# A four-layer graph network: row products summed by VectorE out of PSUM, early blocks' turned sums kept, weighted products in one run

## The chip, the cores and the metric

The kernel runs on one core of a Trainium2 chip. A core has TensorE (PE in the profile, its weight loads PEld), VectorE (DVE), ScalarE (ACT), GpSimd (POOL) and SyncE (SP), whose queue issues most of the transfers. The metric is the device time of one execution in microseconds; lower is better.

## What is computed

The input is x, 3327 nodes of 64 features, and adj, a 3327 x 3327 matrix of weights with many zeros. Four layers follow each other, each of the form x = layernorm(x + f(x)). Layer 1 is a hyperbolic graph layer; for it the part that matters here reads

```python
x_tan = logmap0(x)
adj_att = sigmoid(left + right.T) * adj
x_local = logmap(x[:, None, :], x[None, :, :])
support = einsum('ij,ijd->id', adj_att, x_local)
out = proj(expmap(support, x))            # needs, for each node i, dots such as
x = layernorm(x + out)                    # sum_d x[i,d]*m[i,d] and sum_d m[i,d]**2
```

Here m is a weighted sum over the neighbours. Layer 2 is `x = tanh(concat([adj @ x, x]) @ W)`, twice; layer 3 counts the neighbours of each node and weights the last hundred of them.

## The kernel before

The nodes are padded to 3328 = 26 blocks of 128. Two blocks, one of each half of the nodes, lie side by side as 128 columns, so there are 13 pairs ("slots" 2g and 2g+1 for pair g). `adjT` is streamed from HBM in row blocks of 128 x 3328, 1664 KB each; seven of them stay in SBUF (`kept`).

**near_sphere** is layer 1's main loop: 104 tiles, each with a product on TensorE (L1387), Arctan on ScalarE (L1396), products with the attention on VectorE (L1407 to L1411) and a sum on TensorE (L1431). Its sums go by ScalarE (L1437) into `mT`, node along the free axis. In its last tiles POOL multiplies a half of mT with riT (the rows of x turned, L1614) into xm, and makes small statistics of [128, 26]; TensorE turns blocks 0 to 5 of mT back to node-major, centred, in the PSUM tile pq_early (L1627), whose squares (sq_e) and last columns (t_e) ScalarE takes (L1632, L1636). VectorE makes the other half of xm (L1643) and the row sums of sq_e (L1644).

**near_end** ends layer 1. TensorE turns blocks 6 to 12 (m_and_t, L1702), then sums xm by node with 26 matmuls against but_last, two columns wide, into the PSUM tile pe (p_of, L1722). ScalarE squares the turned blocks (L1716) and copies them into x2 (m_out, L1712). VectorE takes pe (L1768) and runs a long chain of operations on [128, 26], through one Tanh (L1806) and two roots (L1839) on ScalarE, to the factors alpha, beta and beta_c (L1870, L1871, L1880). Meanwhile TensorE turns blocks 0 to 5 once more, and makes x times layer 2's weight (x_w, from w_x) and m times the weight (m_w, from w_m), both by `times` (L1742). `x_out` (L1748) copies x_w into lj by ScalarE. VectorE at last makes lj = alpha * m_w + beta * x_w by groups of blocks (L1877 to L1879: pair 0; pairs 1 to 3; 12; 4 to 7; 8 to 11), then x2 (L1884 to L1886).

**layers** begins with layer 2's first product: for each row block, eight matmuls (16 records) into four PSUM accumulators cnt, taken by turns, two matmuls each (L517, in the order third, first, fourth, second bank of the four). It needs lj of that block and the block's adjT. Four blocks (at_l) are loaded ahead; after them SP's queue has bt_l (one buffer, in the pool `more`), then at_l again. A tile of masks, `carry`, `tm` and `more` lie in SBUF where near_end's tiles lay.

What sets the order: between `tc.manual_schedule` marks each named engine runs its instructions in the order of the program's text; SP's queue runs in its own. Each engine is in order, so an instruction that waits holds everything behind it on that engine. A pool opened with `reuse_waits="tile"` waits tile by tile for what lay in its place. Two engines reading one PSUM tile take turns in the order of the text (L1732's reads follow L1716's squares). PSUM has eight banks: before, four belong to the pool l1w (x_w, m_w and the like), one to l1t (pe), three to l1m (pm); layer 2's accumulators take the upper four.

Of the kernel before, what the change touches and what calls it, by code (L numbers as in the profile page):

```python
# [19 lines left out]
P = 128  # L20
# [62 lines left out]
def kernel(  # L83
# [1093 lines left out]
    with tc.tile_pool(name="l1", bufs=1) as l1:  # L1177

        def l1_stat(name):
            return l1.tile([P, NB], F32, name=name)  # L1180

        aa, g1, ga, xn, rxn, gs, gs2, gk, lpn, aav, gsp = (
            l1_stat(name)
            for name in ("aa", "g1", "ga", "xn", "rxn", "gs", "gs2", "gk", "lpn", "aav", "gsp")
# [104 lines left out]
        def near_sphere(mT, ljT_0, xm, sq_e, t_e):  # L1289
# [3 lines left out]
            with tc.tile_pool(name="n1", bufs=1, reuse_waits="tile") as n1, tc.tile_pool(  # L1293
# [235 lines left out]
                with tc.manual_schedule(  # L1529
# [69 lines left out]
                    for t in range(len(tiles)):  # L1599
# [12 lines left out]
                        if t == len(tiles) - 4:  # L1612
                            of = slice(0, 2 * CW)
                            nc.gpsimd.tensor_tensor(xm[:, of], mT[:, of], riT[:, of], ALU.mult)  # L1614
                            gp = nc.gpsimd

                            gp.tensor_scalar(gs, g1, MIN_NORM, ANGLE_LEAD, ALU.max, ALU.mult)
                            gp.tensor_tensor(gk, gs, ga, ALU.mult)
                            gp.tensor_scalar(gsp, g1, -0.5, None, ALU.mult)
                            gp.tensor_tensor(gsp, gsp, gs, ALU.mult)  # L1620
                            gp.tensor_tensor(gs2, gs, gs, ALU.mult)
                            gp.tensor_scalar(aav, aa, 1.0 / D, LN_EPS, ALU.mult, ALU.add)
# [8 lines left out]
                        if t == len(tiles) - 2:  # L1631
                            nc.scalar.activation(  # L1632
                                sq_e.rearrange("p (a k h) d -> p a k (h d)", a=2, k=3),
                                pm[..., :P], AF.Square,
                            )
                            nc.scalar.copy(  # L1636
                                t_e.rearrange("p (a k h) -> p a k h", a=2, k=3), pm[..., P:]
                            )
                    stt(inv_s, vq[:, 1], -0.5 / 0.9, r2[:, 1], op0=ALU.mult, op1=ALU.mult)
                    stt(rxn, r2[:, 0], -0.5, inv_s, op0=ALU.mult, op1=ALU.mult)  # L1640
                    vec(xn, aa, rxn, ALU.mult)
                    for of in (slice(c * CW, (c + 1) * CW) for c in (2, 3)):
                        vec(xm[:, of], mT[:, of], riT[:, of], ALU.mult)  # L1643
                    nc.vector.tensor_reduce(lpn[:, :12], sq_e, axis=AX.X, op=ALU.add)  # L1644

        def near_end(mT, ljT, xm, t_e, x2):
# [4 lines left out]
            with tc.tile_pool(name="l1e", bufs=1) as l1e, tc.tile_pool(  # L1651
                name="l1w", bufs=4, space=PSUM
            ) as l1w, tc.tile_pool(name="l1t", bufs=1, space=PSUM) as l1t, tc.tile_pool(
# [57 lines left out]
                def m_out(g, n):  # L1711
                    nc.scalar.copy(halves_of(x2[:, slots(g, n)]), m_of(g))  # L1712
# [5 lines left out]
                pe = l1t.tile([P, NBH, 2], F32, name="pe")  # L1718

                def p_of(first, last):  # L1720
                    for k in range(first, last):
                        nc.tensor.matmul(  # L1722
                            pe[:, k], xm[:, k * P : (k + 1) * P], but_last,
                            start=True, stop=True,
                        )
# [27 lines left out]
                p_of(0, NBH)  # L1753
                squares(6, 3)
                squares(9, 3)
                squares(12, 1)
# [10 lines left out]
                p = pe.rearrange("p n h -> p (n h)")  # L1767
                vec(k, p, gs, mul)  # L1768
                vec(gp, p, gsp, mul)
# [7 lines left out]
                m_and_t(0, 3)  # L1777
# [11 lines left out]
                m_and_t(3, 3)  # L1789
                last_x = in_bank("x_w_12")  # L1790
                times(last_x, ljT, w_x, *fours[3])
                ka = of(mul, k, aa, "ka")
# [14 lines left out]
                nc.scalar.copy(w_m, second[:, :P])  # L1807
                warm_e = st("warm")
                nc.scalar.activation(warm_e[:, :1], ones, AF.Sqrt)
                m_out(0, 3)  # L1810
# [33 lines left out]
                x_out(xs[0], *fours[0])  # L1844
                x_out(xs[1], *fours[1])
# [10 lines left out]
                m_out(3, 3)  # L1856
                nc.scalar.copy(w3_dg, second[:, P : 2 * P])
                x_out(last_x, *fours[3])
                rest_x = in_bank("x_w_8")
                mw = {b: in_bank(f"m_w_{b}") for b in (0, 3, 1, 2)}  # L1860
                times(mw[0], mT, w_m, *fours[0])
                times(rest_x, ljT, w_x, *fours[2])
                x_out(rest_x, *fours[2])
                for b in (3, 1, 2):
                    times(mw[b], mT, w_m, *fours[b])
# [232 lines left out]
        with tc.If(n_below == 0) as norms:  # L2098
            with ExitStack() as arm:
                with tc.tile_pool(name="n1m", bufs=1) as n1m:  # L2100
                    mT = n1m.tile([P, HALF], F32, name="mT")
                    ljT_0 = n1m.tile([P, HALF], F32, name="ljT_0")
                    sq_e = n1m.tile([P, 12, D], F32, name="sq_e")
                    t_e = n1m.tile([P, 12], F32, name="t_e")

                    xm = x2.rearrange("p n d -> p (n d)")
                    near_sphere(mT, ljT_0, xm, sq_e, t_e)
                    blocks = blocks_ahead(arm)
                    near_end(mT, ljT_0, xm, t_e, x2)
                layers(x2, xc, True, *blocks)  # L2110
# [43 lines left out]
```

## Time and profile before

| what | us |
|---|---|
| median of three runs (498.72 to 500.65) | 500.58 |
| profiled execution, its own time | 499.99 |
| its span, first to last instruction | 498.2 |
| TensorE busy in the span | 480.3 (96%) |
| VectorE busy | 349.5 (70%) |
| ScalarE busy | 266.1 (53%) |
| POOL busy | 192.1 (39%) |
| near_sphere's last product on VectorE ends (L1409) | 189.4 |
| near_end's chain begins (L1768) | 195.47 |
| layer 2's first matmul (L517) | 205.14 |
| layer 2's first pass ends | 288 |

A line of a timeline gives start, duration, engine, line of the kernel, operation, tiles written and read, shapes, number of instructions merged, and in brackets the idle time before it with what ended it. A line of waits gives who waited for whom, the total, the number of times and the longest. A line of the table by stretch gives, after each engine's busy time, the granted TensorE clock (1.00 is full), the transfers' share of the DMA engines, and GB/s.

### The profile page before, as it was taken

The numbers are of one execution on the slowest core, as the hardware profiler recorded it, in microseconds if no ns is written. First come the engines' busy times: TensorE is split into PE (matmuls) and PEld (weight loads), VectorE is DVE, ScalarE is ACT, GpSimd is POOL, SyncE is SP. The second block draws the span as 40 slices with busy tenths as digits, with TensorE's granted clock in tenths as the row PEclk, the third lists the DMA queues.
The fourth block names the chain that finished last, engine by engine and source line by source line (L and its number), as shares of the span: only waits on it lengthen the run. The fifth ranks groups of instructions, "written<-read, shape, count | busy, mean of one in ns | idle before, by whom it ended". The sixth has DMA issues, their size and how long they took to land. (4 is left out here: it accounts for less than half of the span.)

```text
span 498.2 us, 7727 instructions
## 1 busy us (share of the span) xinstructions
PE 480.3 (96%) x2865; PEld 220.4 (44%) x2865; DVE 349.5 (70%) x602; ACT 266.1 (53%) x377; POOL 192.1 (39%) x171
## 2 busy tenths in 40 slices
PE   7999999999999999999999999999999999999992
PEld 4733333333333338643333353333345554455551
DVE  6788888878888887995363322656239998788744
ACT  4799999999999985300000000000016885657541
POOL 4299999989999991000000000000242154000000
PEclk9799999999999998999999999999999999999996
DMA  9888988887888278899999019998987699949001
GB/s 278 340 284 285 328 265 274 273 272 259 283 274 277 72 285 312 365 402 428 424 425 379 0 22 393 430 362 325 414 337 236 224 331 364 392 162 357 3 1 43
DMA packets 34202, 139.20 MB, mean 279 GB/s; under 512 B 11263, under 2 KB 13041, under 8 KB 29035
## 3 DMA queue, kind: packets, MB, share of 16 engines
q1 hardware_dynamic: 30603, 137.41, 73.8%
q0 software_dynamic: 1216, 0.63, 0.6%
q10 hardware_dynamic: 2336, 0.58, 0.6%
q8 instruction: 24, 0.39, 0.3%
q14 instruction: 23, 0.19, 0.1%
HBM read 136.93 MB, written 1.04 MB: 277 GB/s over the span
## 5 line engine op out<-in xcount | busy, mean ns | idle before, releaser
L1365 POOL TENSOR_TENSOR sg<-sg,at 128x832 f32<-128x832 f32 x88 | 131.4, 1517 | 7.7 <-ACT sg L1360 3.7
L517 PE MATMUL cnt<-at_l,lj 128*64 128x416 f32 x496 | 90.8, 515 | 0.8 <-DMA at_l<-in_adjT 0.8
L1360 ACT ACTIVATE sg<-lb,rb 128x1664 f32<-128x1664 f32 (+1 forms) x53 | 88.1, 1664 | 0.0
L1387 PE MATMUL pq<-riT,ljT 64*128 64x416 f32 x416 | 87.4, 536 | 0.2
L1431 PE MATMUL acc<-v,lj 128*64 128x416 f32 x416 | 85.2, 525 | 0.0
L1396 ACT ACTIVATE pq<-pq 128x832 f32<-128x832 f32 x104 | 83.8, 851 | 1.8 <-issue 1.6
L630 ACT ACTIVATE x<-cnt 128x416 f32<-128x416 f32 x8 | 4.1, 517 | 144.7 <-PE cnt L517 144.7
L669 ACT ACTIVATE w<-cnt 128x416 int16<-128x416 f32 x136 | 63.9, 522 | 25.3 <-PE cnt L651 23.8
L1411 DVE SCALAR_TENSOR_TENSOR v<-pq,sg 128x832 f32<-128x832 f32 x52 | 53.3, 1025 | 19.0 <-ACT pq L1396 18.6
L464 POOL DMA_DIRECT2D t_rows<-tb x4 | 2.7, 720 | 151.0 <-DVE tb L462 151.0
L1387 PEld LDWEIGHTS pq<-riT,ljT 64*128 64x128 f32 x416 | 35.5, 186 | 49.8 <-ACT pq L1396 30.6
L517 PEld LDWEIGHTS cnt<-at_l,lj 128*64 128x64 f32 x496 | 34.3, 137 | 51.0 <-issue 48.4
L882 PE MATMUL acc<-w,s 128*128 128x416 bf16 x208 | 53.1, 339 | 0.0
L1431 PEld LDWEIGHTS acc<-v,lj 128*64 128x64 f32 x416 | 26.1, 136 | 52.3 <-issue 48.2
L667 DVE TENSOR_SCALAR w<-cnt 128x416 int16<-128x416 f32 x72 | 41.6, 587 | 10.0 <-PE cnt L651 7.8
L517 PE MATMUL cnt<-kept,lj 128*64 128x416 f32 x224 | 41.6, 514 | 0.0
L651 PE MATMUL cnt<-mask,tri 128*128 128x416 bf16 x136 | 35.5, 339 | 1.8 <-ACT w L669 0.9
L368 DVE TENSOR_SCALAR mask<-ah 128x1664 bf16<-128x1664 f32 x34 | 35.5, 1060 | 2.3 <-DMA ah<-in_adjT 2.3
L1408 DVE SCALAR_TENSOR_TENSOR pq<-pq,sg 128x416 f32<-128x416 f32 x52 | 31.2, 600 | 1.8
L445 DVE TENSOR_SCALAR tm<-at_l 128x1664 bf16<-128x1664 f32 x16 | 15.7, 1023 | 22.9 <-PE t L452 20.9
L1407 DVE SCALAR_TENSOR_TENSOR v<-pq,sg 128x416 f32<-128x416 f32 x52 | 30.2, 581 | 0.0
L1035 POOL DMA_DIRECT2D out<-hid x1 | 0.5, 502 | 74.5 <-DVE hid L1040 74.5
(320 smaller groups left out, 523.5 us busy)
## 6 DMA issues: line engine op xcount, KB each, us to landing
at_l<-in_adjT SPq DMA_DIRECT2D x27, 1664.0 KB
at<-in_adjT SPq DMA_DIRECT2D x44, 832.0 KB
ah<-in_adjT SPq DMA_DIRECT2D x34, 832.0 KB
kept<-in_adjT SPq DMA_DIRECT2D x7, 1664.0 KB
bt_l<-in_adjT SPq DMA_DIRECT2D x6, 1664.0 KB
lb<-lf_rows SPq DMA_DIRECT2D x2, 384.0 KB
mask<-t_rows SPq DMA_DIRECT2D x34, 3.2 KB
ljT<-ljT SPq DMA_DIRECT2D x4, 128.0 KB
```

Source lines behind the costliest of these rows:

```text
L368: nc.vector.tensor_scalar(mask[q], ahead.pop(q), 0.0, None, ALU.not_equal)
L517: nc.tensor.matmul(acc[c][h * D : (h + 1) * D, :], hw[:, slot(jb), :], blocks[jb][:, o : o + CW], start=c not in begun, stop=last, skip_gr ...
L651: nc.tensor.matmul(cnt[c][e], tri, mask[q][:, of], start=True, stop=True, skip_group_check=True,)
L667: nc.vector.tensor_scalar(to, of, 0.0, None, ALU.max)
L669: nc.scalar.activation(to, of, AF.Relu)
L882: nc.tensor.matmul(acc[h, c][:, e, :], s12[:, slot(jb)].rearrange("p t d -> p (t d)"), ws[q, c, e], start=first, stop=last,)
L1360: nc.scalar.activation(sg[:, :, of], lbs[:, :, of], AF.Sigmoid, bias=rb[:, sl : sl + 1])
L1365: nc.gpsimd.tensor_tensor(sg[:, h, of], sg[:, h, of], at[:, h, of], ALU.mult)
L1387: nc.tensor.matmul(pq[:, h, :], ljT[h != jb // NBH][rows, of], riT[rows, ch * CW : (ch + 1) * CW], start=True, stop=True,)
L1396: nc.scalar.activation(pqs[t], pqs[t], AF.Arctan, bias=ANGLE_FIRST, scale=ANGLE_STEP)
L1411: stt(w, pq, ANGLE_REST, sg, op0=ALU.add, op1=ALU.mult)
L1431: nc.tensor.matmul(accs[cp, ci][h * D : (h + 1) * D, :], lj[:, slot(jb), :], w[:, h, :], start=(jb == orders[cp][0]), stop=(jb == orders[c ...
```

## The change

Four things are changed at the end of layer 1.

The row sums of x times m are no longer made from products of the turned rows by TensorE. VectorE multiplies the node-major m, out of PSUM, with xc and reduces along the row: blocks 0 to 5 at the end of near_sphere (into xm_e, a new tile of 3 KB a partition), the others in near_end with x2 as scratch. The factors gks and gsp take up the node scale s.

The squares of blocks 0 to 5 are summed by POOL in a tree of additions instead of VectorE's reduce.

The turned sums of blocks 0 to 5 are copied into x2 by ScalarE out of pq_early, and not turned a second time.

The pool of weighted products has five PSUM banks instead of four (pe's pool is gone). All of x_w and m_w are written by TensorE in one run; the copies of second_w and of x_w's first four blocks come before Tanh in ScalarE's order, the other copies after it.

```diff
--- before.py
+++ after.py
@@ -1179,9 +1179,11 @@
         def l1_stat(name):
             return l1.tile([P, NB], F32, name=name)
 
-        aa, g1, ga, xn, rxn, gs, gs2, gk, lpn, aav, gsp = (
+        aa, g1, ga, xn, rxn, gs, gs2, gk, lpn, aav, gsp, gks, xms = (
             l1_stat(name)
-            for name in ("aa", "g1", "ga", "xn", "rxn", "gs", "gs2", "gk", "lpn", "aav", "gsp")
+            for name in (
+                "aa", "g1", "ga", "xn", "rxn", "gs", "gs2", "gk", "lpn", "aav", "gsp", "gks", "xms"
+            )
         )
         s, inv_s, gas, lf, rb = (l1_stat(name) for name in ("s", "inv_s", "gas", "lf", "rb"))
 
@@ -1286,7 +1288,7 @@
             sca(aa, g1, -1.0, 1.0, ALU.mult, ALU.add)
         in_order.close()
 
-        def near_sphere(mT, ljT_0, xm, sq_e, t_e):
+        def near_sphere(mT, ljT_0, sq_e, t_e, xm_e, x2):
 
 
 
@@ -1610,14 +1612,13 @@
                         if t == 8:
                             spread_left(7)
                         if t == len(tiles) - 4:
-                            of = slice(0, 2 * CW)
-                            nc.gpsimd.tensor_tensor(xm[:, of], mT[:, of], riT[:, of], ALU.mult)
                             gp = nc.gpsimd
 
                             gp.tensor_scalar(gs, g1, MIN_NORM, ANGLE_LEAD, ALU.max, ALU.mult)
                             gp.tensor_tensor(gk, gs, ga, ALU.mult)
-                            gp.tensor_scalar(gsp, g1, -0.5, None, ALU.mult)
-                            gp.tensor_tensor(gsp, gsp, gs, ALU.mult)
+                            gp.tensor_tensor(gsp, gs, s, ALU.mult)
+                            gp.tensor_tensor(gks, gk, s, ALU.mult)
+                            gp.tensor_scalar(gks, gks, -2.0, None, ALU.mult)
                             gp.tensor_tensor(gs2, gs, gs, ALU.mult)
                             gp.tensor_scalar(aav, aa, 1.0 / D, LN_EPS, ALU.mult, ALU.add)
                         if t == len(tiles) - 3:
@@ -1636,21 +1637,32 @@
                             nc.scalar.copy(
                                 t_e.rearrange("p (a k h) -> p a k h", a=2, k=3), pm[..., P:]
                             )
+                            w = D
+                            while w > 2:
+                                w //= 2
+                                gp.tensor_tensor(
+                                    sq_e[:, :, :w], sq_e[:, :, :w], sq_e[:, :, w : 2 * w], ALU.add
+                                )
+                            gp.tensor_tensor(lpn[:, :12], sq_e[:, :, 0], sq_e[:, :, 1], ALU.add)
                     stt(inv_s, vq[:, 1], -0.5 / 0.9, r2[:, 1], op0=ALU.mult, op1=ALU.mult)
                     stt(rxn, r2[:, 0], -0.5, inv_s, op0=ALU.mult, op1=ALU.mult)
                     vec(xn, aa, rxn, ALU.mult)
-                    for of in (slice(c * CW, (c + 1) * CW) for c in (2, 3)):
-                        vec(xm[:, of], mT[:, of], riT[:, of], ALU.mult)
-                    nc.vector.tensor_reduce(lpn[:, :12], sq_e, axis=AX.X, op=ALU.add)
-
-        def near_end(mT, ljT, xm, t_e, x2):
+
+                    def first(v):
+                        return v[:, :12].rearrange("p (a k h) d -> p a k (h d)", a=2, k=3)
+
+                    vec(first(xm_e), pm[..., :P], first(xc), ALU.mult)
+                    nc.vector.tensor_reduce(xms[:, :12], xm_e, axis=AX.X, op=ALU.add)
+                    nc.scalar.copy(first(x2), pm[..., :P])
+
+        def near_end(mT, ljT, t_e, x2):
 
 
 
             mul, add, sub = ALU.mult, ALU.add, ALU.subtract
             with tc.tile_pool(name="l1e", bufs=1) as l1e, tc.tile_pool(
-                name="l1w", bufs=4, space=PSUM
-            ) as l1w, tc.tile_pool(name="l1t", bufs=1, space=PSUM) as l1t, tc.tile_pool(
+                name="l1w", bufs=5, space=PSUM
+            ) as l1w, tc.tile_pool(
                 name="l1m", bufs=3, space=PSUM
             ) as l1m:
                 sqm = l1e.tile([P, 14, D], F32, name="sq_m")
@@ -1715,14 +1727,9 @@
                     sl = slice(2 * (g - 6), 2 * (g - 6 + n))
                     nc.scalar.activation(halves_of(sqm[:, sl]), m_of(g), AF.Square)
 
-                pe = l1t.tile([P, NBH, 2], F32, name="pe")
-
-                def p_of(first, last):
-                    for k in range(first, last):
-                        nc.tensor.matmul(
-                            pe[:, k], xm[:, k * P : (k + 1) * P], but_last,
-                            start=True, stop=True,
-                        )
+                def x_times_m(g, n):
+                    sl = slots(g, n)
+                    vec(halves_of(x2[:, sl]), m_of(g), halves_of(xc[:, sl]), mul)
 
                 gt, q, k = st("gt"), lpn, st("k")
                 gp = st("gp")
@@ -1750,10 +1757,10 @@
                 m_and_t(6, 3)
                 m_and_t(9, 3)
                 m_and_t(12, 1)
-                p_of(0, NBH)
-                squares(6, 3)
-                squares(9, 3)
-                squares(12, 1)
+                for g, n in ((6, 3), (9, 3), (12, 1)):
+                    x_times_m(g, n)
+                    squares(g, n)
+                nc.vector.tensor_reduce(xms[:, 12:], x2[:, 12:], axis=AX.X, op=add)
                 vec(gt[:, :12], t_e, gk[:, :12], mul)
                 for g, n in ((6, 3), (9, 3), (12, 1)):
                     t_of(g, n)
@@ -1764,9 +1771,8 @@
                 m_out(12, 1)
                 nc.scalar.activation(w3_dg, w3_dg, AF.Copy, scale=float(2**27))
 
-                p = pe.rearrange("p n h -> p (n h)")
-                vec(k, p, gs, mul)
-                vec(gp, p, gsp, mul)
+                vec(k, xms, gks, mul)
+                vec(gp, xms, gsp, mul)
                 vec(k, k, gt, add)
 
                 first = in_bank("first_w")
@@ -1774,7 +1780,6 @@
                 nc.tensor.matmul(
                     first[:, P : 2 * P], center, w2_dg[:, 0, :], start=True, stop=True
                 )
-                m_and_t(0, 3)
                 all_mT, w_m, w_x = (
                     l1e.tile([P, P], F32, name=name) for name in ("all_mT", "w_m", "w_x")
                 )
@@ -1786,9 +1791,16 @@
                 xs = [in_bank(f"x_w_{g}") for g, _ in fours[:2]]
                 times(xs[0], ljT, w_x, *fours[0])
                 times(xs[1], ljT, w_x, *fours[1])
-                m_and_t(3, 3)
                 last_x = in_bank("x_w_12")
                 times(last_x, ljT, w_x, *fours[3])
+                rest_x = in_bank("x_w_8")
+                times(rest_x, ljT, w_x, *fours[2])
+                nc.scalar.copy(w_m, second[:, :P])
+                nc.scalar.copy(w3_dg, second[:, P : 2 * P])
+                x_out(xs[0], *fours[0])
+                mw = {b: in_bank(f"m_w_{b}") for b in (0, 3, 1, 2)}
+                for b in (0, 3, 1, 2):
+                    times(mw[b], mT, w_m, *fours[b])
                 ka = of(mul, k, aa, "ka")
                 gq = of(mul, gs2, q, "gq")
                 u2 = both(gp, -2.0, ka, "u2", mul, add)
@@ -1804,10 +1816,10 @@
                 vec(th, th, xn, mul)
                 arg, th = th, st("tanh")
                 nc.scalar.activation(th, arg, AF.Tanh, scale=-1.0)
-                nc.scalar.copy(w_m, second[:, :P])
                 warm_e = st("warm")
                 nc.scalar.activation(warm_e[:, :1], ones, AF.Sqrt)
-                m_out(0, 3)
+                x_out(xs[1], *fours[1])
+                x_out(last_x, *fours[3])
                 uy = of(mul, th, ux, "uy")
                 y2 = of(mul, th, th, "y2")
                 be = of(mul, th, g2, "be")
@@ -1841,8 +1853,7 @@
                     return r0, r
 
                 r0, r = table_root(root, "on")
-                x_out(xs[0], *fours[0])
-                x_out(xs[1], *fours[1])
+                x_out(rest_x, *fours[2])
 
                 hv = of(mul, root, aav, "hv")
                 stt(hv, n2, 1.0 / D, hv, op0=mul, op1=add)
@@ -1853,16 +1864,6 @@
                 stt(be, r, 0.5, be, op0=mul, op1=add)
                 r0, t = table_root(var, "ln")
                 beg, bes = of(mul, be, g1, "beg"), of(mul, be, s, "bes")
-                m_out(3, 3)
-                nc.scalar.copy(w3_dg, second[:, P : 2 * P])
-                x_out(last_x, *fours[3])
-                rest_x = in_bank("x_w_8")
-                mw = {b: in_bank(f"m_w_{b}") for b in (0, 3, 1, 2)}
-                times(mw[0], mT, w_m, *fours[0])
-                times(rest_x, ljT, w_x, *fours[2])
-                x_out(rest_x, *fours[2])
-                for b in (3, 1, 2):
-                    times(mw[b], mT, w_m, *fours[b])
                 n_r = of(mul, var, t, "n_r")
                 vec(n_r, n_r, t, mul)
                 stt(n_r, n_r, -3.0, t, op0=add, op1=mul)
@@ -2102,11 +2103,11 @@
                     ljT_0 = n1m.tile([P, HALF], F32, name="ljT_0")
                     sq_e = n1m.tile([P, 12, D], F32, name="sq_e")
                     t_e = n1m.tile([P, 12], F32, name="t_e")
-
-                    xm = x2.rearrange("p n d -> p (n d)")
-                    near_sphere(mT, ljT_0, xm, sq_e, t_e)
+                    xm_e = n1m.tile([P, 12, D], F32, name="xm_e")
+
+                    near_sphere(mT, ljT_0, sq_e, t_e, xm_e, x2)
                     blocks = blocks_ahead(arm)
-                    near_end(mT, ljT_0, xm, t_e, x2)
+                    near_end(mT, ljT_0, t_e, x2)
                 layers(x2, xc, True, *blocks)
         with norms.Else():
             with ExitStack() as arm:
```

## The prediction, made before the result was known

> **What bounds the kernel now.** I read the page's tenths first: TensorE is at 9 in nearly every slice, so only time at which TensorE's order is held up counts. The end of layer 1, which the diff touches, lies at 185 to 211 us. The list of waits of the SP queue from 170 to 300 us comes next, then TensorE's waits, then the timelines of each engine there.
>
> ```profile
> SPq L218 <- DVE gsp L1880: 14.9, 1, 14.9
> ```
> ```profile
> PE cnt L517 <- DMA at_l<-in_adjT: 0.8, 1, 0.8
> ```
> ```profile
> 192.48 2.96 PE L1722 MATMUL pe<-but_last,x 128*128 128x2 f32 x26
> ...
> 203.04 2.17 PE L1742 MATMUL m_w<-w_m,mT 128*128 128x128 f32 x18
> 205.14 11.39 PE L517 MATMUL cnt<-at_l,lj 128*64 128x416 f32 x64
> ...
> 221.95 2.96 PE L517 MATMUL cnt<-at_l,lj 128*64 128x416 f32 x16
> 225.74 3.01 PE L517 MATMUL cnt<-at_l,lj 128*64 128x416 f32 x16 [0.82 <-DMA at_l<-in_adjT]
> ```
> ```profile
> 192.21 1.04 ACT L1716 ACTIVATE sq_m<-pm 128x384 f32<-128x384 f32 x3 [0.78 <-DVE x L1643]
> 194.58 0.48 ACT L1712 COPY x<-pm 128x384 f32<-128x384 f32 x1 [1.33 <-PE pe L1722]
> ...
> 197.59 0.23 ACT L1806 ACTIVATE e_tanh<-e_th 128x26 f32<-128x26 f32 x1 [1.06 <-DVE e_th L1804]
> ```
> ```profile
> 195.47 0.19 DVE L1768 TENSOR_TENSOR e_k<-pe,gs 128x26 f32<-128x26 f32 x1 [0.98 <-PE pe L1722]
> ...
> 203.30 0.19 DVE L1870 SCALAR_TENSOR_TENSOR gs<-e_n_r,e_al 128x26 f32<-128x26 f32 x1
> ```
>
> To see: row sums run through TensorE as 26 matmuls two columns wide (192.48 to 195.44); VectorE waits 0.98 for them and starts its chain of small steps at 195.47. Each step waits for the one before, through Tanh at 197.59 and two roots, to alpha at 203.30. 1.1 us after alpha the first block of lj is ready, and layer 2 starts on TensorE at 205.14. From there to 288 TensorE stops once, at 225.74, for a block from HBM: the 16 matmuls before took 3.79 us from start to start where the neighbours take 2.79, so 1.0 is lost. That block was late since SP's queue stood at bt_l until L1880 (210.53) had run. So the term that sets the end is when the chain ends and layer 2 can start, and, up to 1.0 us, when bt_l is issued. From 288 on no transfer is under way, and what follows is released by TensorE: I take a shift there over one for one.
>
> **Removed, and covered.** POOL's product (L1614, 1.95 us) goes; its row is followed by an idle of 15.8 us, so it is worth nothing. POOL gets a tree of six additions of sq_e in its place: L1365's 1.95 for 832 elements and 1.06 for 416 give about 1.0, 0.55 and four of about 0.3, done near 193.3; its reader, gq, comes after 197. Nothing on the path, and nothing below zero either; if that cover were gone, gq would wait. The 26 matmuls (2.96) and the two later turns (0.83 each) leave TensorE, and two eviction copies of 0.46 leave ScalarE, for one of 768 elements earlier.
>
> **VectorE's new order before the chain.** Out: two L1643 (1.29 together) and L1644 (0.94). In: a product of 768 out of PSUM (L1877 has 0.57 for 384, 0.69 for 512: about 0.96), a reduce of 768 (L1644's own shape: 0.94), products of 384, 384 and 128 (0.57, 0.55, 0.30) and a reduce of 896 (0.54 for 384, 0.68 for 512, 0.94 for 768: 1.07). That is 4.4 in and 2.2 out, against the 0.98 of waiting that goes: even with everything ready the chain would start 1.2 later less what can be begun earlier (VectorE idles 0.84 ahead of L1643). It isn't all ready. The product starts when ScalarE has read the same tile (190.21) and ends at 191.2; ScalarE's 768 copy out of that tile comes after it and after mT (191.43), and ends at 192.2 (L1632's shape: 0.81, by the copies' slope 0.75).
>
> Now the added wait. L1702's first turn stood only behind mT (190.78). Its pool takes banks of the pool that holds pq_early. Does it wait for every reader of that pool, or only for its own banks? Bounds: 190.78 and 192.25. The nearest row is L1716 above: sq_m does not lie over riT, and still waits for L1643, the last reader of riT; so a plain pool waits for the whole pool under it. I take 192.25. Behind it queue all the turns: block groups 6, 9 and 12 are ready at 193.2, 193.85 and 194.1 (0.94 for the first, as before, then 0.112 a record).
>
> So: products 193.2 to 194.65, reduce to 195.75, four small products to 196.05, L1760 and L1761 (1.14) to 197.1, and the chain starts at about 197.05 for 195.47: 1.6 late. Its argument for Tanh is there 2.08 later, at 199.15.
>
> **ScalarE and TensorE ahead of Tanh.** x2 is now scratch for the products, so L1712's copies wait for that reduce and the small products: they start at 195.95, where the second one's 195.25 stood before. From there on pitches as before: all_mT 197.35, w_x 197.65. TensorE's second_w starts at 197.44 (0.08 after all_mT, as at 196.34), then x_w's first four blocks. And x_out of those four now stands *ahead* of Tanh in ScalarE's order. At full clock (0.112 a record) they are done at 199.05, the copy (0.57) ends at 199.7 and Tanh starts at 199.6: 2.0 late. At half clock (0.29, then 0.2125, L1784 and L1742 at 196.34 to 199.2) they are done at 200.28 and Tanh starts at 200.83: 3.2 late. Queued behind Tanh on ScalarE are the root table's load and two more copies; by their durations they end 2.6 after Tanh, and the first root needs ScalarE 2.8 after, so nothing more is added there.
>
> Which clock? The row:
>
> ```profile
> 195.00:196.00 1.00, 1.00 (x10) 1.00 (x11) 0.49 (x4) 0.81 (x5) 0.00 (x0) 1.00 0.99 413
> 196.00:197.00 1.00, 1.00 (x8) 0.99 (x7) 0.96 (x9) 0.53 (x3) 0.00 (x0) 0.70 0.99 413
> 197.00:198.00 1.00, 1.00 (x7) 1.00 (x6) 0.71 (x6) 0.39 (x3) 0.00 (x0) 0.50 1.05 434
> ```
>
> The third figure from the end is the granted clock. It fell to half at 196.4, for 3.2 us, after a stretch in which TensorE always had an instruction, but two-column ones. [...] I go with the row, nearly whole: 3.1 late, with 2.0 and 3.25 as the ends.
>
> **From Tanh to layer 2.** The steps between are untouched (6.0 us). The weighted products now come in one run and are off the path: x_w and m_w, 52 records, end near 205, where they ended at 205.2, and alpha comes at 206.4. But PSUM: the products' pool grows from four banks to five, beside three of pm. Layer 2's four accumulators are the upper four banks: they lay over pe and pm, and now one lies over the fifth bank. Banks are given first, then from the last down, then in order of release, so second_w gets the fifth and m_w_0 takes it over. Its last reader is L1879 for blocks 1 to 3, which ended at 206.05. TensorE's second accumulator, reached at 205.89 before, so waits until 206.1 plus the delay: 0.2 more (0 if it lies elsewhere, 0.9 if it is m_w_3).
>
> While TensorE stands from about 205 to 209, but for 0.7 us, the clock can fall again and cost layer 2's start half of up to 3.3 us: 0 to 1.6, I take 0.5 (the stretch before 196.4 held about a third of real work, this one a quarter to a half).
>
> **Loads.** The first four at_l loads wait no longer for L1643, and come over 3 us earlier: nothing, since layer 2 doesn't wait for them. bt_l: layer 1's statistics move up by 3,072 bytes (xm_e) against it. It covers bytes 15,104 to 28,416 of that region; e_n_r and e_bes lay at 25,664 and 25,536 and now lie at 28,736 and 28,608, outside. So SP's queue, and the at_l loads behind bt_l, wait for alpha (206.4) and not for L1880 (213.6): the block of 225.74 is there in time, and the 1.0 us of TensorE's wait goes. From both sides: 0 to 1.2 saved; I take 1.0.
>
> **Sum.** 3.1 + 0.2 + 0.5 - 1.0 = 2.8 us. The profiled execution took 499.99 (span 498.2 and 1.8 around it): 502.8. Its time lies 0.6 under the median of the runs (500.58), so the forecast is 503.4.
>
> **Rivals.**
> - *Full clock* (likely otherwise the same): 2.0 + 0.2 + 0.4 - 1.0 = 1.6: 502.2.
> - *The load pays for the delay; not slower.* If L1702 waits only for its own banks, TensorE's turns start at 190.78, VectorE never stands, the chain starts at 195.95 (0.5 late), and x_out is done by 198.5: Tanh is 0.9 to 1.1 late. With 0.2 for the bank and the 1.0 of the early bt_l: 500.8. It decides where Tanh is less than 0.8 late. For it: the rows show no PSUM pool waiting so. Against it: L1716.
> - *A late bank.* If the fifth bank goes to m_w_1 or m_w_2 (last read at 208.69 and 210.62), layer 2's second accumulator waits 2.6 or 4.5 more: 506.0 to 507.9. Against it: the order of the banks in the trace's program.
> - *bt_l still waits as before* (its region touched by another late reader): the forecast and 1.0: 504.4.
> - *Faster by more than 2.5.* No row offers that much: 1.0 of waiting is all that TensorE has to 288. Left for what I don't see.
>
> **Chances.** Forecast with half clock 0.5 (own range 501.8 to 505.2, the bt_l case in it), full clock 0.18, the load pays 0.15, a late bank 0.11, unseen gain 0.06. A measurement of this kernel can tell about 0.5% (2.5 us) from no change, 498.1 to 503.1. Slower by more: 0.4 of the forecast's 0.5, the late bank, and 0.03 of full clock: 0.54. Within: 0.40. Faster: 0.06. The range 500.2 to 506.4 leaves out the unseen gain, the upper half of the late bank and the low end of the third case.
>
> **What would show it.** Right: L1702's first turn (or its line then) near 192.2 behind ScalarE's copy out of pq_early; e_k near 197; Tanh at 199.6 to 200.9 behind x_out and not behind VectorE; the granted clock at half somewhere in 197 to 203; a gap of 0.9 us in cnt after its first four records, ended by VectorE; bt_l issued at 206 to 207; no wait for at_l near 225. Wrong: turns at 190.8, Tanh below 198.6, or any wait of L517 for m_w past 210.

## The result, and the profile after

The changed kernel takes 503.05 us (median; 501.66 to 504.65), the kernel before 499.44 in the same runs (498.70 to 500.65): ratio 1.0075, 95% interval 1.0057 to 1.0093. The prediction was 503.4, in the range 500.2 to 506.4. The profiled execution of the changed kernel took 503.05, its span 501.3; before it was 499.99 and 498.2. So the pair of profiles differs by 3.1 us, for 2.8 predicted, and the pair of medians by 3.6. The forecast of 503.4 had been set on a median of 500.58 from three runs, which is 1.1 above the one measured here: that it comes so close to 503.05 is in part luck.

Layer 1's loop ended 0.26 earlier in this profile than in that of before. Times below are therefore given twice where it matters: as the trace has them, and "from the loop's end", counted from the start of the loop's last group of eight accumulating matmuls (189.23 before, 188.97 after).

Two lines of TensorE's timeline before, for the comparisons below:

```profile
190.78 1.86 PE L1702 MATMUL pm<-all_m,mT 128*128 128x130 f32 x14
...
216.37 2.96 PE L517 MATMUL cnt<-kept,lj 128*64 128x416 f32 x16
```

TensorE's timeline, changed kernel:

```profile
191.92 1.83 PE L1714 MATMUL pm<-all_m,mT 128*128 128x130 f32 x14 [1.33 <-ACT x L1656]
...
197.12 0.46 PE L1789 MATMUL second_w<-w_dg,all_mT 128*128 128x128 f32 x2 [3.04 <-issue]
...
197.64 4.69 PE L1749 MATMUL x_w<-w_x,ljT 128*128 128x128 f32 x26
202.17 3.07 PE L1749 MATMUL m_w<-w_m,mT 128*128 128x128 f32 x26
206.83 0.92 PE L517 MATMUL cnt<-at_l,lj 128*64 128x416 f32 x4 [1.60 <-DVE lj L1880]
208.57 12.08 PE L517 MATMUL cnt<-at_l,lj 128*64 128x416 f32 x60 [0.82 <-DVE lj L1880]
220.47 2.97 PE L517 MATMUL cnt<-kept,lj 128*64 128x416 f32 x16
...
226.05 5.77 PE L517 MATMUL cnt<-at_l,lj 128*64 128x416 f32 x32
```

ScalarE's timeline there:

```profile
191.06 0.80 ACT L1656 COPY x<-pq_early 128x768 f32<-128x768 f32 x1
...
199.48 0.59 ACT L1755 COPY lj<-x_w 128x512 f32<-128x512 f32 x1 [1.21 <-PE x_w L1749]
199.96 0.23 ACT L1818 ACTIVATE e_tanh<-e_th 128x26 f32<-128x26 f32 x1
```

VectorE's:

```profile
192.96 1.35 DVE L1732 TENSOR_TENSOR x<-pm,xc 128x384 f32<-128x384 f32 x3 [1.04 <-PE pm L1714]
194.35 1.09 DVE L1763 TENSOR_REDUCE xms<-x 128x14 f32<-128x896 f32 x1
...
196.70 0.17 DVE L1774 TENSOR_TENSOR e_k<-xms,gks 128x26 f32<-128x26 f32 x1
...
205.67 0.19 DVE L1871 SCALAR_TENSOR_TENSOR gs<-e_n_r,e_al 128x26 f32<-128x26 f32 x1
```

SP's waits, and the table by stretch, whose third figure from the end is the granted clock:

```profile
SPq L218 <- PE m_w L1749: 13.1, 1, 13.1
SPq L218 <- DVE gs L1871: 0.6, 1, 0.6
```
```profile
198.00:199.00 1.00, 1.00 (x6) 1.00 (x6) 0.75 (x5) 0.27 (x2) 0.00 (x0) 0.50 1.03 439
...
207.00:208.00 1.00, 0.75 (x4) 0.03 (x2) 0.96 (x3) 0.00 (x0) 0.00 (x0) 0.99 1.04 306
208.00:209.00 1.00, 0.43 (x2) 0.32 (x4) 0.97 (x4) 0.00 (x0) 0.00 (x0) 0.50 0.87 346
209.00:210.00 1.00, 1.00 (x5) 0.28 (x3) 1.00 (x3) 0.00 (x0) 0.00 (x0) 0.50 0.93 373
...
211.00:212.00 1.00, 1.00 (x6) 0.33 (x4) 1.00 (x3) 0.00 (x0) 0.00 (x0) 0.80 0.87 359
```

What to see, in order. The first turn stands 1.33 us for ScalarE's copy out of pq_early, with which it shares no data. VectorE stands 1.04 for that turn and starts its chain at 196.70 (195.47 before). Tanh's argument is ready at 198.76, but Tanh runs at 199.96 (197.59 before), directly behind the copy of x_w, and that copy waited 1.21 for TensorE at half clock. Alpha follows at 205.67 (203.30). The second accumulator starts 0.82 after the first one's four records end. The clock falls a second time, for 208.0 to 211.4 (worked out from the 0.99 and 0.80 of the stretches at its ends), so that the first four blocks take 13.64 us from 206.83 to the kept block (11.23 before). And the two blocks at 226.05 run through in 5.77, where before TensorE waited 0.82.

The account of the two profiles, against the prediction's terms:

| term | predicted | measured |
|---|---|---|
| Tanh later (and alpha, by the same) | 3.1 | 2.37 (199.96 - 197.59) |
| fifth bank | 0.2 | 0.31 (second accumulator 208.57 - 205.89 = 2.68, less 2.37) |
| half clock at layer 2's start | 0.5 | 1.42 (220.47 - 208.57 = 11.90 for 10.48) |
| early bt_l | -1.0 | -1.0 (228.85 - 226.05 = 2.80 for 3.79) |
| sum | 2.8 | 3.1 |

The sums agree better than their terms: Tanh's term was 0.7 too large and that of the clock 0.9 too small, and the two errors cancel.

### The profile page after: what moved, and what is told of

Its sections match the earlier page's. It is cut to its first block, busy times and chain, and to the rows that moved or that the text cites. A ratio compares the mean times of both kernels' runs of the same rounds, so it can differ in the third digit from the quotient of the medians.

```text
span 501.3 us, 7655 instructions
## 1 busy us (share of the span) xinstructions
PE 478.1 (95%) x2827; PEld 217.4 (43%) x2827; DVE 351.8 (70%) x605; ACT 266.5 (53%) x376; POOL 194.0 (39%) x177
## 3 DMA queue, kind: packets, MB, share of 16 engines
HBM read 136.93 MB, written 1.04 MB: 275 GB/s over the span
## 5 line engine op out<-in xcount | busy, mean ns | idle before, releaser
L517 PE MATMUL cnt<-at_l,lj 128*64 128x416 f32 x496 | 92.1, 521 | 2.4 <-DVE lj L1880 2.4
L464 POOL DMA_DIRECT2D t_rows<-tb x4 | 4.3, 1545 | 154.0 <-DVE tb L462 154.0
L882 PE MATMUL acc<-w,s 128*128 128x416 bf16 x208 | 53.1, 339 | 0.0
```

What stands on the lines that cost most here:

```text
L517: nc.tensor.matmul(acc[c][h * D : (h + 1) * D, :], hw[:, slot(jb), :], blocks[jb][:, o : o + CW], start=c not in begun, stop=last, skip_gr ...
L882: nc.tensor.matmul(acc[h, c][:, e, :], s12[:, slot(jb)].rearrange("p t d -> p (t d)"), ws[q, c, e], start=first, stop=last,)
```

## The experiments

Eleven kernels, each run beside the kernel before. In the batch of e1, e2, e3 and e5 that one took 499.88, in that of e6 to e9 499.91, in the last one 499.23. The changed kernel has no run in these batches, so they are compared with it by their ratios to the kernel before (its own is 1.0075, 1.0057 to 1.0093). No kernel leaves work out; those with a fill add matmuls whose results nothing reads.

Key times from the loop's end (us), each from its kernel's profile; e1 is Tanh first, e2 the waits by tile, e3 both fills, e7 everything together:

| event | before | after | e1 | e2 | e3 | e7 |
|---|---|---|---|---|---|---|
| first turn | 1.55 | 2.95 | 2.95 | 1.55 | 2.95 | 1.55 |
| chain starts (e_k) | 6.24 | 7.73 | 7.73 | 6.46 | 7.73 | 6.46 |
| Tanh's argument ready | 8.32 | 9.79 | 9.80 | 8.53 | 9.81 | 8.54 |
| x_w's first four done | 9.96 | 10.47 | 10.03 | 9.78 | 9.72 | 8.46 |
| Tanh | 8.36 | 10.99 | 9.83 | 10.29 | 10.24 | 8.58 |
| layer 2's first matmul | 15.91 | 17.86 | 16.70 | 17.16 | 17.11 | 15.45 |
| first kept block | 27.14 | 31.50 | 28.93 | 29.39 | 29.34 | 26.67 |
| block of the old wait | 36.51 | 39.88 | 37.31 | 37.77 | 37.72 | 35.05 |

The loop's end itself is at 189.28 (e1), 189.45 (e2), 187.28 (e3) and 189.06 (e7).

**Does Tanh wait for the copy put ahead of it?** The theory behind the prediction says that two things in line make Tanh late: the pool's wait, then the copy. The rival was that VectorE's longer work alone does it. e1 moves the copy behind Tanh:

```diff
-                x_out(xs[0], *fours[0])
...
                 nc.scalar.activation(warm_e[:, :1], ones, AF.Sqrt)
+                x_out(xs[0], *fours[0])
```

> The changed kernel with one move in ScalarE's order: the copy of x_w's first four blocks comes behind Tanh and the root table's load, with the two others. Theory (the delay is made of waits: 2.4 us at Tanh, 0.3 for the fifth bank, 1.4 for the half clock at layer 2's start, 1.0 given back by the early load): Tanh starts when VectorE's argument is there, 198.8 for 199.96, layer 2 follows 1.2 earlier: about 501.9, ratio 1.005. Rival 'clock' (the loss is the half clock in the two thin stretches, 0.8 and 1.4): Tanh may move, but the x_w run is as slow as before and ends no earlier: 503.0. Rival 'work' (VectorE has 2.2 us more to do ahead of its chain and that is the loss): Tanh waits for that chain, at most 0.2 is gained: 502.9.

Measured: 500.34, ratio 1.0012 (0.9997 to 1.0026). ScalarE, then TensorE:

```profile
199.11 0.23 ACT L1817 ACTIVATE e_tanh<-e_th 128x26 f32<-128x26 f32 x1 [0.53 <-DVE e_th L1815]
...
200.76 1.22 ACT L1755 COPY lj<-x_w 128x512 f32<-128x512 f32 x3
```
```profile
205.98 0.92 PE L517 MATMUL cnt<-at_l,lj 128*64 128x416 f32 x4 [0.43 <-DVE lj L1880]
207.72 10.70 PE L517 MATMUL cnt<-at_l,lj 128*64 128x416 f32 x60 [0.82 <-DVE lj L1880]
```

Tanh now waits for VectorE, 1.16 earlier from the loop's end. That was expected; the rest of the gain was not: TensorE stood 0.43 instead of 1.60 ahead of layer 2, the clock held there, and the 60 records took 10.70 for 12.08.

**Is it the pool's wait?** e2 opens the two PSUM pools so that they wait tile by tile:

```diff
-                name="l1w", bufs=5, space=PSUM
+                name="l1w", bufs=5, space=PSUM, reuse_waits="tile"
...
-                name="l1m", bufs=3, space=PSUM
+                name="l1m", bufs=3, space=PSUM, reuse_waits="tile"
```

> The changed kernel with the two PSUM pools of layer 1's end opened so that they wait tile by tile for what lay in their place; nothing else differs. Theory: the first turn (line 1714) no longer waits for ScalarE's copy out of pq_early and starts at 190.5 for 191.92; the products of x and m follow VectorE's first reduce at 191.9 without the idle of 1.04; the chain starts at 195.5 for 196.70, and second_w, x_w and Tanh follow 1.2 to 1.3 earlier: about 501.8, ratio 1.005. If the clock then stays up through x_w, 0.8 more. Rival 'clock': the idle stretch of TensorE ahead of second_w stays as long (3 us), the half clock stays: 503. Rival 'work': VectorE is busy from 190 on without a stop and gains only the 1.04 of its idle: 502.0, so this run alone does not tell it from the theory.

Measured: 501.78, ratio 1.0027 (1.0004 to 1.0049).

```profile
191.00 1.86 PE L1714 MATMUL pm<-all_m,mT 128*128 128x130 f32 x14
...
197.31 3.96 PE L1749 MATMUL x_w<-w_x,ljT 128*128 128x128 f32 x26
```
```profile
199.26 0.59 ACT L1755 COPY lj<-x_w 128x512 f32<-128x512 f32 x1 [1.27 <-PE x_w L1749]
199.74 0.23 ACT L1818 ACTIVATE e_tanh<-e_th 128x26 f32<-128x26 f32 x1
```

The turn has no wait, and the chain starts 1.27 earlier, 0.22 behind the kernel before. So the pool's wait, not VectorE's work, made nearly all of the chain's 1.49. But Tanh gained only 0.70, for x_w's first four ran at half clock from the start, and the copy ahead of Tanh ended last again.

**What is the half clock worth?** e3 fills two thin stretches of TensorE, ahead of second_w's own matmuls and behind the last m_w:

```diff
+                two = ident.unsqueeze(1).to_broadcast([P, 2, P])
+                for _ in range(6):
+                    nc.tensor.matmul(second[:, 2 * P :], ident, two, start=True, stop=True)
...
+                fill = in_bank("fill_w")
+                for _ in range(3):
+                    nc.tensor.matmul(fill[:, : 2 * P], ident, two, start=True, stop=True)
```

> The changed kernel with idle matmuls that write unread columns: six of 256 columns ahead of second_w, in TensorE's idle stretch from 194.0 to 197.1, and three behind the last product, in the stretch before layer 2. They add nothing to what is computed. Theory: the clock stays at full in both stretches; x_w's first four blocks are done about 0.8 earlier, Tanh at 199.15 for 199.96, and layer 2's first four blocks take 2.8 us each again, 1.4 in all: about 500.9, ratio 1.003. Rival 'clock': the same, and all of the loss but the order: 500.9. Rival 'work': the copy is not what Tanh waits for: no more than the 1.4: 501.6.

Measured: 500.08, ratio 1.0009 (0.9994 to 1.0025).

```profile
192.23 2.76 PE L1791 MATMUL second_w<-ident 128*128 128x256 f32 x12
...
195.95 3.07 PE L1749 MATMUL x_w<-w_x,ljT 128*128 128x128 f32 x26
...
206.12 10.70 PE L517 MATMUL cnt<-at_l,lj 128*64 128x416 f32 x60 [0.81 <-DVE lj L1886]
```

x_w takes 3.07 for 4.69, layer 2's 60 records 10.70 for 12.08, and the granted clock is 1.00 in every microsecond from 190 to 216. Tanh is 0.75 earlier, the block of the old wait 2.16. Work that computes nothing made the kernel faster.

e3a keeps only the first fill, e3b only the second.

> The changed kernel with only the first of the two fills: six idle matmuls of 256 columns ahead of second_w, none behind the last product. Theory (the two half clocks have separate causes, each its own thin stretch): no half clock between 196 and 203, Tanh 0.75 earlier as in the run with both fills, but TensorE still stands for most of 204.5 to 208.5 and the clock falls there for layer 2's first blocks in this run as in the changed kernel: 0.75 of the gain, so 502.2 beside a changed kernel at 503.1. Rival (one drop sets the phase of the next, so that the first fill is enough): as with both fills, 500.1.

> The changed kernel with only the second fill: three idle matmuls of 256 columns behind the last product of m_w, none ahead of second_w. Theory (separate causes): the clock is at half near 198 to 201 as in the changed kernel and Tanh as late as there, and layer 2's first four blocks take 10.5 instead of 11.9: 1.4 less than the changed kernel, 501.7. Rival (the fill is too short a part of the stretch to keep the clock, or the first drop alone matters): 503.1.

Measured: e3a 501.96, ratio 1.0045 (1.0026 to 1.0064); e3b 500.91, ratio 1.0030 (1.0015 to 1.0045). TensorE in e3a:

```profile
205.75 0.92 PE L517 MATMUL cnt<-at_l,lj 128*64 128x416 f32 x4 [2.48 <-DVE lj L1883]
207.48 12.39 PE L517 MATMUL cnt<-at_l,lj 128*64 128x416 f32 x60 [0.82 <-DVE lj L1883]
```

and in e3b:

```profile
204.77 1.46 PE L1807 MATMUL fill_w<-ident 128*128 128x256 f32 x6
206.83 0.92 PE L517 MATMUL cnt<-at_l,lj 128*64 128x416 f32 x4 [0.60 <-DVE lj L1884]
208.57 10.70 PE L517 MATMUL cnt<-at_l,lj 128*64 128x416 f32 x60 [0.82 <-DVE lj L1884]
```

Each fill cures its own stretch and not the other's. e3a has Tanh 0.75 earlier, but the clock falls at 207.6 again; e3b has Tanh no earlier than the changed kernel (11.29 from the loop's end for 10.99) and the 1.4 back at layer 2. The two drops have separate causes; the rival, that the first sets the second, falls. In the medians they save 0.30% and 0.45%, together 0.75%; both fills at once save 0.66%. (The interval of e3a still touches that of the changed kernel.)

**The bank.** e5 goes back to four banks of products (bufs=5 to bufs=4, nothing else).

> The changed kernel with four banks in the pool of the weighted products as before, so that none lies under layer 2's accumulators; m_w then takes the banks of x_w's parts and its last blocks come later (behind the copy of x_w's blocks 8 to 11), near 205.5. Theory: the gap of 0.8 us in cnt after its first four records goes, blocks 0 and 1 follow each other from 206.8; the clock still halves or not as its phase has it: 0.3 to 0.9 faster, 502.4. Rival 'clock': the clock is what slows layer 2's start, with or without that gap: 0.0 to 0.3 faster, 502.9. Rival 'work': 0.3 faster: 502.7.

Measured: 501.03, ratio 1.0018 (1.0004 to 1.0031).

```profile
207.44 13.09 PE L517 MATMUL cnt<-at_l,lj 128*64 128x416 f32 x64 [2.07 <-DVE lj L1880]
```

The 64 records are one run: the gap of 0.82 behind the first four is gone, so it was the bank. The median fell by more than that: 0.57%, some 2.8 us, for 0.6 expected. This profile doesn't explain it: the clock falls twice in it as in the changed kernel, and its first kept block is only 0.25 earlier from the loop's end. Why e5's median fell so far stays open.

**What is the early load worth?** e6 gives it to the kernel before, by writing bes and n_r over tiles that are dead by then:

```diff
-                beg, bes = of(mul, be, g1, "beg"), of(mul, be, s, "bes")
+                beg, bes = of(mul, be, g1, "beg"), lf
+                vec(bes, be, s, mul)
...
-                n_r = of(mul, var, t, "n_r")
+                n_r = rb
+                vec(n_r, var, t, mul)
```

> The kernel before with two of layer 1's small tiles (bes and n_r) written over tiles that are dead by then, so that nothing under bt_l is read after alpha. Theory: bt_l is issued near 205.3 instead of 210.8, TensorE's wait of 0.8 for at_l goes and with it the slower block ahead of it, 1.0 us in all: 498.9 where the kernel before has 499.9 in the same runs, ratio 0.998. Rival (the wait is moved to a later block, or the at_l loads are bound by HBM): no difference.

Measured: 498.75, ratio 0.9981 (0.9961 to 1.0000).

```profile
222.00 5.76 PE L517 MATMUL cnt<-at_l,lj 128*64 128x416 f32 x32
```

bt_l is issued at 205.33 for 210.80, the wait of 0.8 is gone, and the block behind it comes 0.99 earlier from the loop's end. The median is 0.95 lower by its ratio, with an interval that ends at 1.0000. e8 takes the early load away from e1, by giving bes a tile of its own ahead of near_end's turns, so that it lies under bt_l:

```diff
+                bes = st("bes")
...
-                beg, bes = of(mul, be, g1, "beg"), of(mul, be, s, "bes")
+                beg = of(mul, be, g1, "beg")
+                vec(bes, be, s, mul)
```

> As e1_tanh_first (the copy of x_w's first four blocks behind Tanh), but bt_l's bytes lie again over a tile that is read last by L1881, so that the load waits for that step as in the kernel before. Everything else, the product and reduce on VectorE too, is as in e1. Theory (the early load is worth about 1 us): bt_l is issued about 7 us later than in e1, near 8 us after alpha, the block that TensorE needed at the old wait lands some 0.7 to 1.0 after TensorE gets there, a wait of L517 for at_l comes back, and the time is 0.7 to 1.0 over e1's: about 501.1. Rival (the early load is worth nothing in the changed kernel, since TensorE comes there later anyway): the same as e1, 500.3, and no wait for at_l.

Measured: 502.26, ratio 1.0050 (1.0032 to 1.0068). TensorE:

```profile
223.83 2.99 PE L517 MATMUL cnt<-at_l,lj 128*64 128x416 f32 x16
228.05 3.01 PE L517 MATMUL cnt<-at_l,lj 128*64 128x416 f32 x16 [1.23 <-DMA at_l<-in_adjT]
```

The two executions agree within 0.05 us up to 223.8, half clock included, so this is the load alone: bt_l at 212.35 for 205.69, and 4.22 from start to start for 2.79, 1.43 lost. The medians differ by 1.9. In the two profiles the rest, 0.44, comes in the last layer: from its first matmul (L882) to VectorE's last product (L1040) it takes 108.18 in e8 and 107.74 in e1, and in the thirteen profiles anything from 107.35 to 108.59, so it is not put down to the load. e4 makes e8's edit on the changed kernel itself.

> The changed kernel with bt_l's bytes again over a tile that L1881 reads last; nothing else is changed. In e8 the same edit on top of e1 cost 1.9. Theory (the early load and the half clock at layer 2's start overlap: in the changed kernel TensorE comes to the old wait 2.3 later than in e1, about when the block lands even with the late load): a wait for at_l of 0.3 or less in a profile in which the clock falls at layer 2's start, 503.1 to 503.5 by the median. Rival (the two add up as in the prediction's sum): 1.0 or more over the changed kernel, 504.1 to 505.

Measured: 502.70, ratio 1.0068 (1.0048 to 1.0088); the changed kernel's is 1.0075.

```profile
226.12 2.98 PE L517 MATMUL cnt<-at_l,lj 128*64 128x416 f32 x16
229.81 3.02 PE L517 MATMUL cnt<-at_l,lj 128*64 128x416 f32 x16 [0.71 <-DMA at_l<-in_adjT]
```

The median shows no cost, as the theory of an overlap has it, but the two intervals together leave room for 1.0; the profile has a wait of 0.71, twice what I expected at most, and costs 0.9 from start to start. So only the direction is settled, by these two profiles. In e8 the late block is there 23.20 after alpha and TensorE 21.77 after it; in e4 the block 23.41 and TensorE 22.51 (226.12 + 2.79 - 206.40); in the changed kernel TensorE comes 23.18 after alpha. The slower layer 2 starts, the less the early load is worth.

**All together.** e7 is the changed kernel with e1's, e2's and e5's edits; e9 is e7 with six fill matmuls ahead of second_w and four behind the last m_w.

> The changed kernel with three edits together: the two products' PSUM pools wait for the tiles under them alone (first turn 1.4 earlier), the copy of x_w's first four blocks behind Tanh, and four banks of products instead of five. Theory (the delay of the chain is made of the pool's wait, of that copy and of the bank, and the early load then pays for what is left): VectorE's chain 0.2 later than in the kernel before, Tanh within 0.3 of the time at which the argument is ready, so 0.2 to 0.5 after the kernel before's, second accumulator without a wait for L1880, minus 1.0 for the load: 499.3 if the clock holds at layer 2's start, up to 1.4 more if it falls there. Rival (the copies behind Tanh hold up m_w and with it layer 2's start): as e1, 500.3 or more, with m_w's end after alpha.

> As e7_all, with six idle matmuls of 256 columns ahead of second_w and four behind the last product of m_w, whose results nothing reads, so that TensorE has no thin stretch in layer 1's end. Theory (the half clock is caused by thin stretches of TensorE's work): granted clock 0.98 or more from 185 to 215, layer 2's first four blocks in 10.5 or less; 498.5 to 499.3, and a narrower spread than e7. Rival (the clock falls whatever TensorE does there, or the fill delays real work): the same as e7 or more.

Measured: e7 498.32, ratio 0.9968 (0.9952 to 0.9985); e9 497.88, ratio 0.9960 (0.9941 to 0.9979). TensorE in e7:

```profile
190.61 1.86 PE L1714 MATMUL pm<-all_m,mT 128*128 128x130 f32 x14
...
196.46 3.07 PE L1749 MATMUL x_w<-w_x,ljT 128*128 128x128 f32 x26
199.90 3.17 PE L1749 MATMUL m_w<-w_m,mT 128*128 128x128 f32 x26 [0.38 <-ACT lj L1755]
204.51 11.39 PE L517 MATMUL cnt<-at_l,lj 128*64 128x416 f32 x64 [1.44 <-DVE lj L1880]
```

and in e9:

```profile
203.46 1.89 PE L1808 MATMUL pm_fill<-ident 128*128 128x256 f32 x8
205.28 11.39 PE L517 MATMUL cnt<-at_l,lj 128*64 128x416 f32 x64
```

Both beat the kernel before. In e7 the chain is 0.22 behind it, but layer 2 starts 0.46 earlier, since m_w is done at 203.07 and TensorE waits for VectorE's lj alone, and the early load adds its 1.0: the block of the old wait comes 1.46 earlier. The rival (m_w held up by the copies behind Tanh) falls: 0.38 us. In e7's profile the clock did not fall here either, so e9's fill shows only in the runs: its mean clock was 0.987 (0.984 to 0.990) for e7's 0.984 (0.980 to 0.987). Their times can't be told apart, and e9's spread is not narrower (496.67 to 499.60 for 497.28 to 499.99), as I had expected it to be. e9's fill ends a little after lj is ready: its first matmul in layer 2 waits for nothing, but is 0.2 later than e7's from the loop's end.

## Why the prediction was right, point by point

*The pool's wait.* Right: the first turn was to come at 192.25 behind the copy out of pq_early; it came at 191.92, or 192.18 on the clock of before. e2 shows the cause: 1.40 gone with the waits by tile.

*VectorE's order.* Right: e_k was to come 1.6 late and came 1.49 late from the loop's end. Here e2 sharpens it: of these 1.49 only 0.22 is VectorE's new work, though the durations summed to 1.2. (The prediction had allowed for 0.84 of them to be begun earlier, which leaves 0.4.) The new products and reduces fit nearly whole into time in which VectorE had waited for the turns and for the two-column sums. POOL's tree was done at 193.06, for 193.3 expected, and its reader gq came at 197.23.

*The copy ahead of Tanh, at half clock.* Right in kind: Tanh ran behind the copy, not behind VectorE. The delay was put at 3.1 between ends of 2.0 and 3.25. That 3.1 was my own estimate, and no profile of the changed kernel shows it; it measured 2.37 in its place (2.63 from the loop's end), because the clock fell at 197.7, when x_w began, and not ahead of second_w: 199.44 for the first four, between the 199.05 and 200.28 worked out. e4 and e5 show the later end: there the clock fell 0.5 to 0.75 earlier from the loop's end, and Tanh came 3.21 and 3.11 late from the loop's end. Going with the row, in which the clock fell behind a stretch without a gap (TensorE busy for all of 195 to 196), was right: of the two drops the first came after an idle of 3.04 us, the second with no idle longer than 1.60 ahead of it. The row itself was read a little short: the half clock of before lasted 3.42, from 196.40 to 199.82, not 3.2.

*The fifth bank.* Right: 0.31 for 0.2; e5 takes the gap away.

*Half clock at layer 2's start.* The one term mis-sized: 0.5 predicted inside 0 to 1.6, 1.42 measured, nearly the whole. I took the stretch from 205 to 209 for less than thin enough, with 0.7 us of work in it. In e3b's profile, with 1.5 us of fill matmuls there, the clock held, and in e1's, with 1.16 us less of standing. But 1.42 is what one execution paid: in e2's profile the clock held too, where TensorE stood 2.43 us ahead of layer 2. The medians of the changed kernel and of e3b differ by 0.45%, some 2.2 us; how often the clock falls there stays open.

*The load.* Right in size in this pair (1.0) and in the kernel before (e6: 1.0). What the sum missed is that its terms don't stand apart: a load whose time is set by VectorE alone costs 1.43 when it is late and TensorE comes early (e8), and less where the half clock makes TensorE late too (0.9 in e4's profile). So 1.42 for the clock and -1.0 for the load are one account, and only their sum is firm.

*The rivals.* "The load pays for the delay" needed a first turn at 190.78: it didn't happen in the changed kernel and is what e7 makes of it, with the copy moved as well. "A late bank" and "bt_l as before" don't show. The working at full clock (502.2, or 1.6 later) is not what this profile has; e3 is that case. Its profile has the block of the old wait 1.2 later than before, which is the 1.6 without the 0.4 for layer 2's start, where TensorE then loses nothing. Its ratio of 1.0009 (0.5 us) lies lower still, with 1.2 just inside its interval.

## What to carry to other kernels

Before sizing moved work by its durations, ask which waits it inherits: here two orderings (a pool that waits for a neighbour's last reader, a copy written ahead of the step on the path) cost over two microseconds (Tanh comes 2.41 earlier in e7, where both are gone), while VectorE's added work cost 0.22. Where work leaves TensorE next to a stretch in which it stands already, price the clock behind that stretch as well, and try a few matmuls there whose results nothing reads. And don't add a saved transfer wait to a delay of the engine that waits: the later the engine comes, the less there is to save.

## What was not expected of the hardware

The granted clock fell at 196.40 in the kernel before, 0.96 after 26 two-column matmuls that ran without a gap (192.48 to 195.44), and at 207.98 in the changed kernel, behind 2.7 us with 0.9 us of matmuls in them (205.2 to 208.0). At the end of layer 1 it stayed at half for 3.40 to 3.42 us each time, 13 times in ten of the thirteen profiles (worked out from the shares of 1-us stretches, as above): in the kernel before from 196.40 to 199.82, in the changed kernel from 197.74 to 201.16 and from 207.98 to 211.40.

How long TensorE stands doesn't by itself settle whether the clock falls. e2 leaves TensorE idle for 3.13 us ahead of second_w, e7 for 3.14. In e2's profile the clock fell 2.6 us into that, at 195.78:

```profile
193.00:194.00 1.00, 0.20 (x2) 0.00 (x1) 0.96 (x3) 1.00 (x3) 0.43 (x2) 1.00 1.13 319
194.00:195.00 1.00, 0.00 (x0) 0.00 (x0) 1.00 (x6) 0.19 (x2) 0.00 (x0) 1.00 0.78 306
195.00:196.00 1.00, 0.00 (x0) 0.00 (x0) 1.00 (x3) 1.00 (x5) 0.00 (x0) 0.89 0.97 413
196.00:197.00 1.00, 0.67 (x3) 0.70 (x4) 0.96 (x9) 0.50 (x3) 0.00 (x0) 0.50 0.97 413
```

In e7's it didn't fall:

```profile
193.00:194.00 1.00, 0.00 (x0) 0.00 (x0) 0.96 (x2) 0.64 (x3) 0.16 (x1) 1.00 1.02 346
194.00:195.00 1.00, 0.00 (x0) 0.00 (x0) 1.00 (x7) 0.55 (x2) 0.00 (x0) 1.00 1.03 439
195.00:196.00 1.00, 0.06 (x1) 0.09 (x1) 0.97 (x6) 1.00 (x5) 0.00 (x0) 1.00 1.02 426
196.00:197.00 1.00, 1.00 (x9) 1.00 (x10) 0.97 (x9) 0.45 (x3) 0.00 (x0) 1.00 0.98 413
```

Nor does TensorE's work in the stretch. In the changed kernel the four microseconds from 204 to 208 hold 2.15 us of it, and the clock fell at 207.98:

```profile
204.00:205.00 1.00, 1.00 (x12) 1.00 (x10) 0.77 (x6) 0.58 (x2) 0.00 (x0) 1.00 1.00 426
205.00:206.00 1.00, 0.23 (x3) 0.04 (x1) 0.89 (x8) 0.93 (x1) 0.19 (x2) 1.00 1.00 426
206.00:207.00 1.00, 0.17 (x2) 0.17 (x4) 0.93 (x4) 0.00 (x0) 0.00 (x0) 1.00 1.03 426
207.00:208.00 1.00, 0.75 (x4) 0.03 (x2) 0.96 (x3) 0.00 (x0) 0.00 (x0) 0.99 1.04 306
208.00:209.00 1.00, 0.43 (x2) 0.32 (x4) 0.97 (x4) 0.00 (x0) 0.00 (x0) 0.50 0.87 346
```

In e2 the same four hold 1.10 us of it, and the clock stayed at 1.00 in every microsecond from 200 to 216:

```profile
204.00:205.00 1.00, 0.18 (x2) 0.00 (x0) 0.78 (x6) 0.80 (x2) 0.19 (x2) 1.00 1.00 426
205.00:206.00 1.00, 0.00 (x0) 0.00 (x0) 0.91 (x6) 0.71 (x1) 0.00 (x0) 1.00 1.00 426
206.00:207.00 1.00, 0.39 (x2) 0.20 (x4) 0.93 (x4) 0.00 (x0) 0.00 (x0) 1.00 1.00 426
207.00:208.00 1.00, 0.53 (x4) 0.00 (x0) 0.97 (x3) 0.00 (x0) 0.00 (x0) 1.00 1.00 386
```

What decides between such cases no run here shows. So a fill is worth what its runs showed: in e3b's profile 1.5 us of fill matmuls went with a clock that held at layer 2's start, in e3a's 2.8 us with one that held through x_w, and the medians were 0.45% and 0.30% lower. At second_w e7's clock held with no fill; e2's, with the same idle, did not.
